# Chunked attention in a fused f32 layer: value products in quarters of the TensorE array, masked scores kept without zero blocks

## Chip, cores and metric

The kernel runs on one core of a Trainium2 chip. The time is the device time of one execution in microseconds (us); the time before is the median of three runs, 514.29 us (513.94 to 514.57).

## What is computed

One layer over 4 x 2048 = 8192 tokens of 256 features: attention inside chunks of 32 tokens, with a decaying causal mask and a gate, a residual and layer norm, then a gated feed-forward part with integer weights, a residual and layer norm again. Cut to what matters:

```python
Q = x @ W_q.T; K = x @ W_k.T; V = x @ W_v.T
mask = jnp.where(diff >= 0, decay ** diff, 0)          # 32 x 32, diff = i - j
S = jnp.einsum('bncd,bnkd->bnck', Qc, Kc) * mask       # per chunk of 32 tokens
O = jnp.einsum('bnck,bnkd->bncd', S, Vc).reshape(B, T, D)
gate = jax.nn.sigmoid(x @ W_g.T)
out = gate * O @ W_o.T + x
x = _layernorm(x + out)
h = silu(x @ wg.T) * (x @ wu.T);  x = _layernorm(x + h @ wd.T)
```

## The kernel before

**Tiling.** The tokens are worked in 16 blocks of 512 (`TB`), each 4 groups (`NG`) of 128 tokens. A group is two pairs (`PAIR` = 64 tokens), and a pair is two chunks of 32. Features lie in two halves of 128 (`KD`). Queries and keys are folded: `m` = W_q^T W_k, so the scores need only y = m x and x.

**Attention of one block.** `split_gate`, `split_y` and `split_v` make the gate, y and v by three products of split operands each (a high part, a low part, and a "gap" part after ScalarE has scaled the PSUM bank in place, line 540). `attn_scores` (L651) makes, for each group and feature half, two products of 128 rows x 64 columns: pair 0 into partitions 0 to 63 of the PSUM bank `ps`, pair 1 into 64 to 127. Then VectorE multiplies by the mask (L663), one operation for each half of the partitions. The result goes into the diagonal 64x64 blocks of `sT`, a tile of 128 x 4 x 128, of which there are two, used in turn; their off-diagonal blocks were zeroed once at the start (L282, GpSimd) and stay zero. `attn_values` (L673) makes, for each feature half `dc` and group, one product of the full array: v (128 tokens x 128 features) stationary, `sT` (128 tokens x 128 columns, half of them zero) moving. The bank `po` of one `dc` holds 512 tokens, and VectorE gates it into `goT[:, dc, :]` (L682) as soon as its four products are done, while PE makes the other `dc`. `token_parts` then makes the high part of goT (ScalarE, L479), the low part (GpSimd, L480) and, later, the gap part (VectorE, L486), and `split_out` multiplies by W_o (L521) and adds the residual (L744). The first block takes `attn_residual` instead (L704, L728).

**Feed-forward of one block.** `ffn_up` makes for each of six hidden chunks of 128 the products `fg` and `fu` (L833); ScalarE makes s = silu (L842), VectorE u = fu s (L853), ScalarE its high part (L858), GpSimd the low part (L859). `ffn_down` (L704 or L907) multiplies by the down weights. Between the two parts, normalized h is transposed by 32x32 blocks on VectorE (L785) and 16 DMAs of SyncE's queue (L792).

**Order.** The order on each engine is written out by hand: `in_turn` and `in_steady_turn` keep instructions in program order. Loop iteration b (b = 0 to 13) runs the feed-forward of block b beside the attention of block b + 2 and the v, y and gate products of block b + 3. On PE, in an iteration with all parts: hidden chunk 0, chunk 1, scores, chunk 2, v (high and low), chunk 3, v gap, **values**, y (high and low), chunks 4 and 5, y gap, gate (high and low), out (high and low), gate gap, out gap, down. On ScalarE after chunk 3: v copy, normalization of an earlier block (L433), go_hi, scaling of y. Blocks 0 and 1 have their values in the prologue; the last block's come in iteration 13, after which ScalarE has go_hi at once. PSUM has eight banks of 512 f32 per partition, handed out in turn by `bank`.

A second path, `wide_group`, runs only if a weight is too large for the split; with these inputs it doesn't run.

Of the kernel before, what the change touches and what calls it, by code (L numbers as in the profile page):

```python
# [47 lines left out]
F32 = mybir.dt.float32  # L48
# [4 lines left out]
ALU = mybir.AluOpType  # L53

P = 128
CHUNK = 32
PAIR = 2 * CHUNK
SQ = 32
TB = 512
NG = TB // P  # L60
# [16 lines left out]
def kernel(  # L77
# [15 lines left out]
    nc = tc.nc  # L93
    NT, D = x.shape
    H = ffn_gT.shape[1]
    KD = D // P
# [4 lines left out]
    const = ctx.enter_context(tc.tile_pool(name="const", bufs=1))  # L101
    setup = ctx.enter_context(tc.tile_pool(name="setup", bufs=2))
    xin = ctx.enter_context(tc.tile_pool(name="xin", bufs=2))
    work = ctx.enter_context(tc.tile_pool(name="work", bufs=2))
# [9 lines left out]
    def in_turn(ins):  # L114
        tc.keep_in_program_order(ins)

    def bank(name):
        return psum.tile([P, TB], F32, tag="ps", name=name)
# [73 lines left out]
    for n in WARM:  # L192
        nc.tensor.matmul(
            pi[:, :n],
            lhsT=nc.const_aps.tensor(0.0, [P, P]),
            rhs=nc.const_aps.tensor(0.0, [P, n]),
            start=True,
            stop=True,
# [56 lines left out]
    mask = const.tile([P, NG, PAIR], F32, tag="mask", name="mask")  # L255
    nc.vector.memset(mask, 0.0)

    def make_mask():
# [11 lines left out]
        for g in range(P // CHUNK):  # L270
# [5 lines left out]
                    chunk_mask[rows, :].unsqueeze(1).to_broadcast([CHUNK, NG, CHUNK]),  # L276
                )
            )

    sTs = [const.tile([P, NG, P], F32, tag=f"sT_{i}", name=f"sT_{i}") for i in range(2)]  # L280
    for sT in sTs:
        nc.gpsimd.memset(sT, 0.0)  # L282


    def integers(w, w_int, name):

# [46 lines left out]
    def in_steady_turn(ins):  # L333
        if steady:
            tc.keep_in_program_order(ins)
# [307 lines left out]
    def attn_scores(b, yT):  # L643
        xt = xTs.pop(b)
        halves = [slice(i * PAIR, (i + 1) * PAIR) for i in range(P // PAIR)]
        ps = bank(f"ps_{b}")[:, : NG * PAIR].rearrange("p (g c) -> p g c", c=PAIR)
        for g in range(NG):
            for fc in range(KD):
                for rows in halves:
                    tokens = slice(g * P + rows.start, g * P + rows.stop)  # L650
                    product = nc.tensor.matmul(  # L651
                        ps[rows, g, :],
                        lhsT=xt[:, fc, tokens],
                        rhs=yT[:, fc, tokens],
                        start=(fc == 0),
                        stop=(fc == KD - 1),
                    )
                    in_turn(product)
        sTs.append(sTs.pop(0))
        sT = sTs[-1]  # L660
        for rows in halves:
            in_steady_turn(
                nc.vector.tensor_tensor(sT[rows, :, rows], ps[rows], mask[rows], ALU.mult)  # L663
            )
        return sT.rearrange("p g c -> p (g c)")

    def attn_values(b, sT, v, sg):
        goT = work.tile([P, KD, TB], F32, tag="goT", bufs=1, name=f"goT_{b}")
        for dc in range(KD):
            po = bank(f"po_{b}_{dc}")  # L670
            for g in range(NG):
                cols = slice(g * P, (g + 1) * P)
                product = nc.tensor.matmul(  # L673
                    po[:, cols],
                    lhsT=v[:, g, dc * P : (dc + 1) * P],
                    rhs=sT[:, cols],
                    start=True,
                    stop=True,
                )
                in_turn(product)  # L680
            in_steady_turn(
                nc.vector.scalar_tensor_tensor(  # L682
                    goT[:, dc, :], sg[:, dc, :], 1.0, po, ALU.add, ALU.mult
                )
            )
        return goT
# [275 lines left out]
    sg, gate = attn_gate(0)  # L962
# [9 lines left out]
    v, copies = attn_v(0, with_m)  # L972
# [18 lines left out]
    sT = attn_scores(0, yT)  # L991
# [5 lines left out]
    goT = attn_values(0, sT, v, sg)  # L997
# [299 lines left out]
    def wide_group(start, weights):  # L1297

        wide_g, wide_u, wide_d = weights
        tokens = bass.ds(start, P)  # L1300

        def features(pool, tag, name):
            bufs = {"bufs": 1} if tag == "goT" else {}
            return pool.tile([P, KD, TB], F32, tag=tag, name=f"{name}_w", **bufs)[:, :, :P]

        def row(pool, tag, name):
            return pool.tile([P, NG, D], F32, tag=tag, name=f"{name}_w")[:, 0, :]

        def products(pb, pairs):
            for i, (lhsT, rhs) in enumerate(pairs):  # L1310
                nc.tensor.matmul(
                    pb, lhsT=lhsT, rhs=rhs, start=(i == 0), stop=(i == len(pairs) - 1)
                )
            return pb

        def part(dc):
            return slice(dc * P, (dc + 1) * P)

        xt = features(xin, "xT", "xT")
        nc.gpsimd.dma_start(xt, xT[:, tokens].rearrange("(k p) t -> p k t", p=P))  # L1320
        xn = row(xin, "x", "x")
        nc.gpsimd.dma_start(xn, x[tokens, :])
        sg, yT, goT, hT = (
            features(pool, tag, tag)
            for pool, tag in ((work, "sg"), (work, "yT"), (work, "goT"), (moved, "hT"))
        )
        for dc in range(KD):
            pg = products(
                bank(f"pg_w_{dc}")[:, :P],
                [(given["wg"][:, ec, part(dc)], xt[:, ec, :]) for ec in range(KD)],  # L1330
            )
            nc.scalar.activation(sg[:, dc, :], pg, AF.Tanh, scale=HALF)
            py = products(
                bank(f"py_w_{dc}")[:, :P],
                [(given["m"][:, ec, part(dc)], xt[:, ec, :]) for ec in range(KD)],
            )
            nc.vector.tensor_copy(yT[:, dc, :], py)
        v = row(work, "v", "v")
        pv = products(
            bank("pv_w")[:, :D], [(xt[:, ec, :], given["wv"][:, ec, :]) for ec in range(KD)]  # L1340
        )
        nc.vector.tensor_copy(v, pv)
        sT = sTs[-1]
        ps = bank("ps_w")[:, :PAIR]
        for i in range(P // PAIR):
            rows = slice(i * PAIR, (i + 1) * PAIR)
            products(ps[rows, :], [(xt[:, fc, rows], yT[:, fc, rows]) for fc in range(KD)])
            nc.vector.tensor_tensor(sT[rows, 0, rows], ps[rows, :], mask[rows, 0, :], ALU.mult)
        for dc in range(KD):
            po = products(bank(f"po_w_{dc}")[:, :P], [(v[:, part(dc)], sT[:, 0, :])])  # L1350
            nc.vector.scalar_tensor_tensor(
                goT[:, dc, :], sg[:, dc, :], 1.0, po, ALU.add, ALU.mult
            )
        h = row(norm, "h", "h")
        pa = products(
            bank("pa_w")[:, :D], [(goT[:, ec, :], given["wo"][:, ec, :]) for ec in range(KD)]
        )
        nc.vector.tensor_tensor(h, pa, xn, ALU.add)

        def normed(r, name, on_r=1.0):  # L1360
            st = small.tile([P, 6], F32, tag="st", name=f"st_{name}")
            mv = no_moments(name)
            nc.vector.bn_stats(st, r)
            nc.vector.bn_aggr(mv[:, 0, :], st)
            rstd = root(mv, name, on_r, groups=[0])
            nc.vector.reciprocal(rstd[:, :1], rstd[:, :1])
            nc.vector.tensor_scalar(
                r, r, mv[:, 0, 0:1], rstd[:, :1], ALU.subtract, ALU.mult
            )

        normed(h, "aw", HALF)
        nc.vector.tensor_scalar(h, h, 1 / HALF, None, ALU.mult)
        for dc in range(KD):
            pt = bank(f"pt_w_{dc}")[:, :P]
            nc.tensor.transpose(pt, h[:, part(dc)], ident)
            nc.scalar.copy(hT[:, dc, :], pt)
        uT = []
        for hc in range(KH):
            pg, pu = (
                products(  # L1380
                    bank(f"{name}_w_{hc}")[:, :P],
                    [
                        (w[hc * P // D][:, dc, hc * P % D : hc * P % D + P], hT[:, dc, :])
                        for dc in range(KD)
                    ],
                )
                for name, w in (("fg", wide_g), ("fu", wide_u))
            )
            s = work.tile([P, TB], F32, tag="s", name=f"s_w_{hc}")[:, :P]
            nc.scalar.activation(s, pg, AF.Silu)  # L1390
            u = acts.tile([P, TB], F32, tag="u_hi", name=f"u_w_{hc}")[:, :P]
            nc.vector.tensor_tensor(u, pu, s, ALU.mult)
            uT.append(u)
        r = row(work, "r2", "r2")
        rows = [piece[:, k, :] for piece in wide_d for k in range(TB // D)]
        pd = products(bank("pd_w")[:, :D], list(zip(uT, rows)))
        nc.vector.tensor_tensor(r, pd, h, ALU.add)
        normed(r, "fw")
        nc.gpsimd.dma_start(out[tokens, :], r)
# [77 lines left out]
```

## Time and profile before

| | |
|---|---|
| median of three runs | 514.29 us |
| the profiled execution | 515.19 us |
| its span, first to last instruction | 513.6 us |
| granted TensorE clock | 0.999 |
| value products (L673) | 256 records, 31.2 us busy |
| score products (L651) | 512 records, 18.4 us busy |
| masking (L663) | 32 operations, 13.0 us busy |
| gating (L682) | 32 operations, 22.0 us busy |

The profile is one execution. PE is TensorE's matmuls, PEld its weight loads, DVE VectorE, ACT ScalarE, POOL GpSimd, SPq the DMA queue of SyncE. A group's line gives line, engine, operation, output<-inputs, shapes and count, then busy time and mean duration in ns, then the idle time of the engine just before these instructions and what ended it. Matmuls are pipelined: a record's duration is longer than its share of the path, which the chain of work shows better. The chain gives start, length, and engine, tile and line of what the end waited for. A timeline line gives start, length, engine, line, operation, output<-inputs, shapes, count and, in brackets, the idle time before.

### The profile page before, as it was taken

To read this page: it belongs to the slowest core of one execution; us is meant where nothing else is said; L and a number is where in the kernel's file an instruction comes from. 1 tells how busy PE (TensorE), PEld (TensorE's weight loads), DVE (VectorE), ACT (ScalarE), POOL (GpSimd) and SP (SyncE) were. 2 spreads that over 40 slices of the span, in tenths; PEclk is the share of its full clock that TensorE was granted. 3 is DMA by queue.
4 is the path that set the end of the run, shared out by engine and by line. 5 is a ranking of instruction groups with operands and counts; after the bars stand their busy time and mean duration, and the time that the engine had idled before them with its cause. 6 is when DMAs were issued, how large, how long until landed. Compare 5 with 4: busy or idle time off the path is not lost.

```text
span 513.6 us, 9691 instructions
## 1 busy us (share of the span) xinstructions
PE 503.7 (98%) x3480; PEld 399.4 (78%) x3480; DVE 309.3 (60%) x725; ACT 373.1 (73%) x701; POOL 292.2 (57%) x324
## 2 busy tenths in 40 slices
PE   9999899999999999999999999999999999999995
PEld 5788677788878879787787878778787787877684
DVE  3977667564564647547474564647547464665654
ACT  4868686676868777686786868777686786766845
POOL 2835546554746557465464846557465564657764
PEclk9999999999999999999999999999999999999999
DMA  7720312112222122222212222122222211103112
GB/s 243 235 84 20 94 25 82 42 43 68 73 74 74 43 78 88 60 64 83 83 43 71 84 61 75 45 77 86 61 64 82 83 44 30 54 14 98 35 36 69
DMA packets 43315, 36.83 MB, mean 72 GB/s; under 512 B 4865, under 2 KB 39169, under 8 KB 43265
## 3 DMA queue, kind: packets, MB, share of 16 engines
q1 hardware_dynamic: 42144, 35.28, 22.9%
q10 hardware_dynamic: 1120, 0.92, 0.6%
q8 instruction: 28, 0.46, 0.4%
q14 instruction: 23, 0.18, 0.1%
HBM read 20.45 MB, written 8.39 MB: 56 GB/s over the span
## 4 chain that ended last, share of the span: by engine, by line
PE 74%; DVE 8%; ACT 7%; SPq 4%; issue 3%; POOL 2%; DMA 1%; DVEq 0%; ACTq 0%; POOLq 0%
PE fg L833 13%; PE fu L833 12%; PE fdn L704 11%; PE p_y L499 7%; PE p_g L499 7%; PE p_v L521 6%; PE p_o L521 6%; PE po L673 5%; SPq L792 4%; DVE u L853 3%; PE ps L651 2%; ACT s L842 2%; ACT h L433 1%; PE fdn L907 1%; DMA out_dram<-r 1%
## 5 line engine op out<-in xcount | busy, mean ns | idle before, releaser
L859 POOL TENSOR_TENSOR u_lo<-u,u_hi 128x512 f16<-128x512 f32 (+1 forms) x98 | 128.7, 1315 | 100.9 <-ACT u_hi L858 100.9
L853 DVE SCALAR_TENSOR_TENSOR u<-fu,s 128x512 f32<-128x512 f32 (+1 forms) x98 | 66.6, 680 | 127.1 <-ACT s L842 103.7
L858 ACT CAST u_hi<-u 128x512 fp32r<-128x512 f32 (+1 forms) x98 | 59.9, 612 | 85.0 <-DVE u L853 84.9
L833 PE MATMUL fg<-hT_hi,fg_hi 128*128 128x512 f32 (+1 forms) x196 | 71.1, 444 | 0.0
L842 ACT ACTIVATE s<-fg 128x512 f32<-128x512 f32 (+1 forms) x98 | 56.8, 580 | 6.3 <-PE fg L833 6.2
L833 PE MATMUL fu<-hT_hi,fu_hi 128*128 128x512 f32 (+1 forms) x196 | 60.6, 390 | 0.0
L833 PE MATMUL fg<-hT_lo,fg_lo 128*128 128x512 f16 (+1 forms) x196 | 58.2, 378 | 0.0
L833 PE MATMUL fu<-hT_lo,fu_lo 128*128 128x512 f16 (+1 forms) x196 | 57.4, 375 | 0.0
L480 POOL TENSOR_TENSOR go_lo<-goT,go_hi 128x512 fp32r<-128x512 f32 x30 | 38.7, 1313 | 26.3 <-ACT go_hi L479 26.3
L480 POOL TENSOR_TENSOR x_lo<-xT,x_hi 128x512 fp32r<-128x512 f32 x30 | 38.3, 1298 | 24.2 <-ACT x_hi L479 18.0
L744 DVE TENSOR_TENSOR h<-p_o,x 128x512 f32<-128x512 f32 x30 | 19.3, 686 | 42.5 <-PE p_o L521 32.4
L704 PE MATMUL fdn<-fd_hi,u_hi 128*128 128x256 f32 x312 | 44.7, 285 | 0.0
L833 PEld LDWEIGHTS fu<-hT_hi,fu_hi 128*128 128x128 f32 x196 | 36.5, 188 | 8.5
L833 PEld LDWEIGHTS fg<-hT_hi,fg_hi 128*128 128x128 f32 x196 | 34.7, 189 | 9.5
L704 PEld LDWEIGHTS fdn<-fd_hi,u_hi 128*128 128x128 f32 x312 | 39.0, 188 | 0.3
L433 ACT ACTIVATE h<-h,shift_h,scale_h 128x256 f32<-128x256 f32 x52 | 27.0, 590 | 16.8 <-POOL shift_h L396 16.8
L704 PE MATMUL fdn<-fd_lo,u_lo 128*128 128x256 f16 x312 | 38.6, 273 | 0.0
L810 POOL TENSOR_TENSOR hT_lo<-hT,hT_hi 128x512 f16<-128x512 f32 x28 | 35.5, 1290 | 3.7 <-ACT hT_hi L809 3.7
L833 PEld LDWEIGHTS <-fu_lo 128*128 128x128 f16 x196 | 19.2, 98 | 22.4 <-issue 0.3
L673 PE MATMUL po<-sT,v 128*128 128x128 f32 x256 | 31.2, 275 | 0.3 <-DVE sT L663 0.3
L704 PEld LDWEIGHTS <-u_lo 128*128 128x128 f16 x312 | 28.4, 98 | 3.9
L673 PEld LDWEIGHTS po<-sT,v 128*128 128x128 f32 x256 | 30.0, 192 | 0.7 <-PE p_v L521 0.5
(176 smaller groups left out, 1067.2 us busy)
## 6 DMA issues: line engine op xcount, KB each, us to landing
x<-in_x_dram SPq DMA_DIRECT2D x16, 512.0 KB, 3.5
xT<-in_xT_dram SPq DMA_DIRECT2D x15, 512.0 KB, 3.7
hT<-sq SPq DMA_DIRECT2D x224, 32.0 KB, 1.9
out_dram<-r SPq DMA_DIRECT2D x13, 512.0 KB, 3.1
out_dram<-r SPq DMA_DIRECT2D x7, 128.0 KB, 1.7
fg_int<-in_ffn_gT_dram SPq DMA_DIRECT2D x3, 256.0 KB, 7.0
fu_int<-in_ffn_uT_dram SPq DMA_DIRECT2D x3, 256.0 KB, 7.2
fd_int<-in_ffn_dT_dram SPq DMA_DIRECT2D x3, 256.0 KB, 5.9
```

Of the source, the lines that this page charges most:

```text
L433: nc.scalar.activation(r[:, g, :], r[:, g, :], AF.Identity, bias=shift[:, g : g + 1], scale=scale[:, g : g + 1],)
L480: in_turn(nc.gpsimd.tensor_tensor(lo[:, k, :], t[:, k, :], whole, ALU.subtract))
L499: nc.tensor.matmul(pb, lhsT=a[kind][:, k, i * P : (i + 1) * P], rhs=b[kind][:, k, :], start=kind + k == 0, stop=True, skip_group_check=True,)
L521: nc.tensor.matmul(pb[:, j * D : (j + 1) * D], lhsT=b[kind][:, k, g * P : (g + 1) * P], rhs=a[kind][:, k, :], start=kind + k + j == 0, sto ...
L673: product = nc.tensor.matmul(po[:, cols], lhsT=v[:, g, dc * P : (dc + 1) * P], rhs=sT[:, cols], start=True, stop=True,)
L704: product = nc.tensor.matmul(pb[:, j * D : (j + 1) * D], lhsT=part[:, g * P : (g + 1) * P], rhs=w, start=(i == 0), stop=(i == len(terms) - 1),
L810: nc.gpsimd.tensor_tensor(in_order[1], whole, in_order[0].bitcast(F32), ALU.subtract)
L833: product = nc.tensor.matmul(pb, lhsT=w[kind][:, dc, hc * P : (hc + 1) * P], rhs=hT[kind][:, dc, cols], start=(kind == kinds[0] and dc == ...
L842: in_turn(nc.scalar.activation(s, pg, AF.Silu, scale=SCALE / H_UP))
L853: nc.vector.scalar_tensor_tensor(u, pu, U_UP / H_UP, s, ALU.mult, ALU.mult)
L858: in_steady_turn(nc.scalar.copy(hi, u))
L859: nc.gpsimd.tensor_tensor(lo, u, hi.bitcast(F32), ALU.subtract)
```

## The change

The value products use quarters of the array. Token rows 0 to 63 of a group (pair 0) and rows 64 to 127 (pair 1) are multiplied apart, and each again for the two 64-feature halves of a feature half: four products of 64 rows x 64 columns, moving 64 columns, where one of 128 x 128 with 128 moving columns stood. Pair 0 writes one PSUM bank and pair 1 another, each bank holding both feature halves of its tokens: 8 blocks of 64 columns. The masked scores are a tile of 128 x 4 x 64 without zero blocks, written by one operation, from the pool `work` with two buffers; the two `sT` tiles and their zeroing go. The gating operation now takes one bank, that is both feature halves of one pair of every group, and writes `goT` in runs of 64. The path that doesn't run is changed in the same way.

```diff
-    sTs = [const.tile([P, NG, P], F32, tag=f"sT_{i}", name=f"sT_{i}") for i in range(2)]
-    for sT in sTs:
-        nc.gpsimd.memset(sT, 0.0)
...
-        sTs.append(sTs.pop(0))
-        sT = sTs[-1]
-        for rows in halves:
-            in_steady_turn(
-                nc.vector.tensor_tensor(sT[rows, :, rows], ps[rows], mask[rows], ALU.mult)
-            )
-        return sT.rearrange("p g c -> p (g c)")
+        sT = work.tile([P, NG, PAIR], F32, tag="sT", name=f"sT_{b}")
+        in_steady_turn(nc.vector.tensor_tensor(sT, ps, mask, ALU.mult))
+        return sT
+
+    def by_pairs(t):
+        return t.rearrange("p k (g r c) -> p (k g) r c", g=NG, c=PAIR)
+
+    def value_products(banks, v, sT, groups, order):
+        for dc in range(KD):
+            for g in groups:
+                for r, po in enumerate(banks):
+                    rows = slice(r * PAIR, (r + 1) * PAIR)
+                    for c in range(P // PAIR):
+                        dims = slice(c * PAIR, (c + 1) * PAIR)
+                        product = nc.tensor.matmul(
+                            po[dims, dc * len(groups) + g, :],
+                            lhsT=v[rows, g, dc * P + dims.start : dc * P + dims.stop],
+                            rhs=sT[rows, g, :],
+                            start=True,
+                            stop=True,
+                        )
+                        order(product)
 
     def attn_values(b, sT, v, sg):
         goT = work.tile([P, KD, TB], F32, tag="goT", bufs=1, name=f"goT_{b}")
-        for dc in range(KD):
-            po = bank(f"po_{b}_{dc}")
-            for g in range(NG):
-                cols = slice(g * P, (g + 1) * P)
-                product = nc.tensor.matmul(
-                    po[:, cols],
-                    lhsT=v[:, g, dc * P : (dc + 1) * P],
-                    rhs=sT[:, cols],
-                    start=True,
-                    stop=True,
-                )
-                in_turn(product)
+        banks = [
+            bank(f"po_{b}_{r}").rearrange("p (n c) -> p n c", c=PAIR)
+            for r in range(P // PAIR)
+        ]
+        value_products(banks, v, sT, range(NG), in_turn)
+        for r, po in enumerate(banks):
             in_steady_turn(
                 nc.vector.scalar_tensor_tensor(
-                    goT[:, dc, :], sg[:, dc, :], 1.0, po, ALU.add, ALU.mult
+                    by_pairs(goT)[:, :, r, :], by_pairs(sg)[:, :, r, :], 1.0, po, ALU.add, ALU.mult
                 )
             )
         return goT
```

More of the change, by code (lines that the diff above doesn't have):

```diff
@@ L1342, in wide_group @@
         nc.vector.tensor_copy(v, pv)
-        sT = sTs[-1]
+        sT = work.tile([P, NG, PAIR], F32, tag="sT", name="sT_w")
         ps = bank("ps_w")[:, :PAIR]
@@ L1347, in wide_group @@
             products(ps[rows, :], [(xt[:, fc, rows], yT[:, fc, rows]) for fc in range(KD)])
-            nc.vector.tensor_tensor(sT[rows, 0, rows], ps[rows, :], mask[rows, 0, :], ALU.mult)
-        for dc in range(KD):
-            po = products(bank(f"po_w_{dc}")[:, :P], [(v[:, part(dc)], sT[:, 0, :])])
+        nc.vector.tensor_tensor(sT[:, 0, :], ps, mask[:, 0, :], ALU.mult)
+        banks = [
+            bank(f"po_w_{i}")[:, :P].rearrange("p (n c) -> p n c", c=PAIR)
+            for i in range(P // PAIR)
+        ]
+        value_products(banks, v.unsqueeze(1), sT, range(1), free)
+        for i, po in enumerate(banks):
+            of_pair = slice(i * PAIR, (i + 1) * PAIR)
             nc.vector.scalar_tensor_tensor(
-                goT[:, dc, :], sg[:, dc, :], 1.0, po, ALU.add, ALU.mult
+                goT[:, :, of_pair], sg[:, :, of_pair], 1.0, po, ALU.add, ALU.mult
             )
```

## The prediction

> **What bounds the kernel now.** I read the page's busy shares first, then its chain of work that ended last, then that chain in a window of one loop iteration, then the groups of instructions by form, then the timelines where TensorE (PE) waits.
>
> ```profile
> PE 503.7 (98%) x3480; PEld 399.4 (78%) x3480; DVE 309.3 (60%) x725; ACT 373.1 (73%) x701; POOL 292.2 (57%) x324
> ...
> PE 74%; DVE 8%; ACT 7%; SPq 4%; issue 3%; POOL 2%; DMA 1%; DVEq 0%; ACTq 0%; POOLq 0%
> ```
>
> PE is the bound: nearly always busy and three quarters of the chain, at a granted clock of 0.999. A microsecond taken from PE in the loop is a microsecond of the span, unless another engine is late next. The chain in one iteration (start, length, what):
>
> ```profile
> 116.28 0.47 PE fu L833 x2
> 116.75 1.08 PE ps L651 x32
> 117.83 0.66 PE fg L833 x2
> 118.49 0.46 PE fu L833 x2
> ...
> 124.55 1.78 PE po L673 x16
> 126.33 1.86 PE p_y L499 x8
> ```
>
> The value products (po) stand on the path for 1.78 us per block. The scores (ps) already use half-width tiles, and give the price I need.
>
> ```profile
> L673 PE MATMUL po<-sT,v 128*128 128x128 f32 x256 | 31.2, 275 | 0.3 <-DVE sT L663 0.3
> L682 DVE SCALAR_TENSOR_TENSOR goT<-sg,po 128x512 f32<-128x512 f32 x32 | 22.0, 687 | 11.2 <-PE po L673 11.0
> L651 PE MATMUL ps<-yT,xT 128*64 128x64 f32 x512 | 18.4, 225 | 0.0
> L663 DVE TENSOR_TENSOR sT<-ps,mask 64x256 f32<-64x256 f32 x32 | 13.0, 406 | 0.4 <-issue 0.2
> ```
>
> Each f32 product leaves two records: 8 value products a block leave 16, 16 score products leave 32. A value record (128 moving columns) costs 1.78/16 = 0.111 us. A score record has half the columns, so one after another 32 would cost 32 x 0.056 = 1.78. They took 1.08: the start stamps come two by two, 6 to 7 ns apart, one pair every 58 ns. So the two column halves of the array run at the same time, and 16 rounds of 58 ns are 0.93. The rest of the 1.08, 0.15, is the way into the tiled mode; the way out is in the next row, where two fg records take 0.66 against 0.46 to 0.47 elsewhere: 0.20. A tiled stage costs its rounds plus 0.35.
>
> **What the Trainium skill says.** "TensorEngine Tiling (Array Packing)", Key Properties: a change of tiling mode drains the engine, and tiles load and multiply independently. The trace agrees: the 0.35 above, and the pairs. The same page, Gotcha 1: PSUM Pressure: different row tiles must write different banks; the edit has one bank per token half, so it obeys; no run here shows two row tiles. "TensorE: Matmul & The Clock Gate", Part 3, Measured speedup vs the span model: tiles of one round start about 4 ns apart and packing by rows and columns composes. The trace has 6 to 7 ns for columns, nothing for rows. "Runtime: NRT & Kernel Launch", Instruction fetch mechanics: an issue floor of about 20 cycles per instruction. The scores hold 4 instructions (two loads, two products) in 58 ns, 14.5 ns each; whether a faster pace lasts is not shown.
>
> **The change part by part.**
>
> *Products.* Removed: 16 records of 0.111. Added: 8 x 4 = 32 products, 64 records of 64 columns in quarter tiles. Four different quarters follow one another in program order, so a round has four records: 16 rounds of 58 ns are 0.93, plus 0.02 for two more starts, plus 0.35 of mode changes that po did not have: 1.30. Gain 1.78 - 1.30 = 0.48 per block. Bounds: at best the mode changes are half hidden, 1.12 (gain 0.66); at worst no row overlap, priced below.
>
> *Masking (L663).* Two 64x256 operations (0.85 together on the timeline) become one 128x256; other 128x256 rows on DVE take 0.40 to 0.41, so I take 0.42 and save 0.43 a block. Mostly DVE is idle anyway, but twice the masking stands in front of PE:
>
> ```profile
> 35.54 0.85 DVE L663 TENSOR_TENSOR sT<-ps,mask 64x256 f32<-64x256 f32 x2
> 36.53 2.02 PE L673 MATMUL po<-sT,v 128*128 128x128 f32 x16 [0.31 <-DVE sT L663]
> ```
>
> In block 1 the gap from the last record to po is 0.589 against 0.118 usually: 0.47 lost, 0.43 of it comes back. And in the loop, masking delays u, so u_hi, so ACT's scaling of p_v, which PE needs:
>
> ```profile
> 335.85 0.30 DVE sT L663
> 336.17 0.43 DVE sT L663
> 336.63 0.70 DVE u L853
> 337.35 0.62 ACT u_hi L858
> 337.97 0.49 ACT p_v L540
> 338.51 1.22 PE p_v L521 x8
> ```
>
> The gap ahead of the p_v gap products is 0.235 where nothing is late; it is 1.06, 0.58 and 0.31 at 91, 338 and 400 us (2.01 at 59 us, where sT is not in the chain). Cutting 0.43 from each gives back 0.43 + 0.34 + 0.07 = 0.84; I take 0.8 (bounds 0 and 0.9).
>
> *Gating (L682).* Still two operations of 512 per block. Each now walks eight runs of 64; the masking rows also write runs of 64 and cost no more than contiguous 256-element rows (406 against 401 to 413 ns), so 0.69 each (at most 0.75). But each reads a token half of all features, and its bank is full only with the last products: neither can start under the products, as the first did. Gating begins about 0.25 after the last product: 0.15 + 0.95 + 0.25 = 1.35 after po's start, and ends at 1.35 + 2 x 0.69 = 2.7; before it ended at 2.67 (124.39 to 127.06). go_hi of the first feature half, which needed only the first operation, now needs both. In the loop ACT reaches go_hi at 128.55, behind normalization, so this costs nothing. In block 0 the output products (L704) follow one product group later and now wait for gating: gain 0. In the last block ACT waits for gating already:
>
> ```profile
> 458.66 1.46 DVE L682 SCALAR_TENSOR_TENSOR goT<-sg,po 128x512 f32<-128x512 f32 x2
> 460.16 0.63 ACT L479 ACTIVATE go_hi<-goT 128x512 fp32r<-128x512 f32 x1 [0.16 <-DVE goT L682]
> 460.83 0.60 ACT L842 ACTIVATE s<-fg 128x512 f32<-128x512 f32 x1
> 461.52 0.69 DVE L853 SCALAR_TENSOR_TENSOR u<-fu,s 128x512 f32<-128x512 f32 x1 [1.39 <-ACT s L842]
> ```
>
> There both go_hi casts start after the second gating, so s, queued behind them, and its user u slip by about 0.47, and the chain runs on from u to a PE wait at 472: cost 0.5 instead of a gain (bounds 0 and 0.5).
>
> *What is late next.* PE arrives 0.48 earlier at the p_g gap products, where ACT's scaling had about 0.29 to spare and the shorter masking gives most of 0.43 more. One iteration (259 us) already stalls there. I charge 0.3 in all (bounds 0 and 1.3, 0.1 in each of 13 iterations).
>
> *Nothing else.* The two zeroing memsets (0.55 each on POOL at 2 to 3 us) lie under the input transfers. The second bank is needed 0.9 earlier; its earlier user, the score bank, was read some 3 us before. No DMA moves. The branch for wide integers does not run.
>
> Sum: 13 loop blocks x 0.48 = 6.2; block 1, 0.48 + 0.43 = 0.9; p_v waits 0.8; last block -0.5; p_g -0.3. Together 7.1. The profiled execution took 515.19 (span 513.6 and 1.6 around it), so 508.1; the median shown, 514.29, is 0.9 below that execution: **507.2**.
>
> **The rivals.**
>
> *Row halves take turns* (slower). The scores show only column halves side by side. If the two row halves alternate, there are 32 rounds of 58 ns: 1.86 + 0.35 = 2.21, 0.43 more than now. 13 x 0.43 = 5.6, block 1 even, last block 0.9, less 0.8 from the masking: +5.7, **520.0**. It decides once the stage exceeds 1.78, that is (1.78 - 0.35)/64 = 22 ns per record, before the masking's gain. For it: 29 ns per score record is the fastest lasting pace in the trace. Against: stamps 6 ns apart, and the skill's packing.
>
> *Instruction supply limits.* 128 loads and products must issue in 0.95. At 18 ns per record, midway between 14.5 and 22, the stage is 1.15 + 0.35 = 1.50, gain 0.28: 3.6 + 0.7 + 0.8 - 0.7 - 0.1 = 4.3, **510.0**.
>
> *A wait takes the place.* ACT's order from p_v to p_g is nearly closed; if PE stalls for half of what it gains in each iteration, 7.1 - 3.1 = 4.0, **510.3**.
>
> **How the numbers follow.** The likeliest case 0.65 (own range 504.5 to 509.5: both best bounds, half the mode cost hidden, give 7.1 + 13 x 0.18 + 0.5 = 10; the worst bounds of the small terms give 5), supply 0.10, wait 0.06, row halves 0.17, and 0.02 for a break-even between them. The likeliest case, supply, wait and break-even hold 0.8 within 504.5 to 514.5; the row case is left out. Faster by over 0.2% (1 us, about what a measurement of this kernel can tell from no change) 0.80, within it 0.03, slower 0.17.
>
> **What would show it.** Right: po as 64 records of 64x64 in about 1.1 us from first to last, starts in fours every 58 ns, the first p_y product about 0.1 late; masking as 16 operations of about 420 ns; iterations near 30.1 us instead of 30.6; both gating operations after the last product. Wrong: starts in pairs (row case), even spacing of 18 ns or more (supply), or new PE gaps ahead of the p_g or p_o gap products (wait). A gating operation much over 0.69, or mode changes costlier for quarters than for halves, would also break the sum.

## The result, and the profile after

The changed kernel takes 507.8 us (median of four runs, 506.66 to 508.91), against 514.29 before: a ratio of 0.9874, 95% interval 0.9847 to 0.9901. Its profiled execution took 507.07 us with a span of 505.5. The page of the profile after, its busy shares and its chain that ended last:

```profile
PE 493.7 (98%) x4248; PEld 387.0 (77%) x4248; DVE 301.1 (60%) x709; ACT 373.1 (74%) x701; POOL 291.4 (58%) x322
...
PE 69%; ACT 5%; DVE 4%; POOL 2%; SPq 2%; issue 2%; DMA 1%; DVEq 0%; ACTq 0%; POOLq 0%
```

PE is still the bound, with 10 us less of work and 768 more records. The groups by form, of after:

```profile
L688 DVE SCALAR_TENSOR_TENSOR goT<-sg,po 128x512 f32<-128x512 f32 x32 | 20.6, 684 | 16.1 <-PE po L670 16.1
L670 PE MATMUL po<-sT,v 64*64 64x64 f32 x1024 | 18.6, 221 | 0.0
L646 PE MATMUL ps<-yT,xT 128*64 128x64 f32 x512 | 18.4, 225 | 0.0
...
L655 DVE TENSOR_TENSOR sT<-ps,mask 128x256 f32<-128x256 f32 x16 | 6.3, 392 | 0.0
```

Gating costs the same per operation (684 ns against 687) though it walks runs of 64. Masking is 16 operations of 392 ns. The value products are 1024 quarter records, 64 a block. How a block's stage lies on PE, from the timeline of after:

```profile
212.11 1.10 PE L516 MATMUL p_v<-wv_gap,x_gap 128*128 128x256 f32 x8
213.14 1.16 PE L670 MATMUL po<-sT,v 64*64 64x64 f32 x64
214.23 0.73 PE L494 MATMUL p_y<-x_hi,m_hi 128*128 128x512 f32 x2
```

The stage takes 1.16 us from its first record to the end of its last. The steps between start stamps inside it, in ns, from the block at 243.22 us (the first seven rounds of the sixteen):

```
7 7 6 87 | 7 7 6 38 | 7 7 6 39 | 6 7 7 38 | 7 6 7 38 | 7 7 6 39 | 6 7 7 38
```

Four quarters start 6 to 7 ns apart, and from the second round on a round of four lasts 58 ns. From the last p_v record ahead of the stage to the third p_y record behind it, PE spends 1.875 us, against 2.362 before: 0.487 less.

The same trace by stretches, each counted between the first records of two score stages (the first score stage began 21.87 us after the span's start before, and 20.48 after):

| stretch | before | after | gain |
|---|---|---|---|
| scores of block 1 to those of block 2 | 19.28 | 18.53 | 0.75 |
| iteration b = 0 | 32.54 | 33.58 | -1.04 |
| b = 1 | 31.81 | 30.55 | 1.26 |
| b = 2 | 30.63 | 30.87 | -0.24 |
| an undisturbed later iteration | 30.61 | 30.07 | 0.54 |
| scores of block 2 to those of block 15 | 400.43 | 394.17 | 6.26 |
| from there to the end | 60.88 | 61.15 | -0.27 |

Two iterations are longer than before. That was the first thing to explain.

### The profile page after: what moved, and what is told of

Its sections match the earlier page's. It is cut to its first block, busy times and chain, and to the rows that moved or that the text cites. A ratio compares the mean times of both kernels' runs of the same rounds, so it can differ in the third digit from the quotient of the medians.

```text
span 505.5 us, 11205 instructions
## 1 busy us (share of the span) xinstructions
PE 493.7 (98%) x4248; PEld 387.0 (77%) x4248; DVE 301.1 (60%) x709; ACT 373.1 (74%) x701; POOL 291.4 (58%) x322
## 4 chain that ended last, share of the span: by engine, by line
PE 69%; ACT 5%; DVE 4%; POOL 2%; SPq 2%; issue 2%; DMA 1%; DVEq 0%; ACTq 0%; POOLq 0%
PE fg L839 14%; PE fu L839 13%; PE fdn L710 12%; PE p_y L494 6%; PE p_g L494 6%; PE p_o L516 6%; PE p_v L516 6%; PE po L670 2%; PE ps L646 2%; DVE u L859 2%; SPq L798 2%; PE fdn L913 1%; ACT s L848 1%; ACT h L428 1%; ACT u_hi L864 1%
## 5 line engine op out<-in xcount | busy, mean ns | idle before, releaser
L688 DVE SCALAR_TENSOR_TENSOR goT<-sg,po 128x512 f32<-128x512 f32 x32 | 20.6, 684 | 16.1 <-PE po L670 16.1
L839 PEld LDWEIGHTS <-fg_lo 128*128 128x128 f16 x196 | 14.0, 98 | 20.9 <-issue 12.9
## 6 DMA issues: line engine op xcount, KB each, us to landing
x<-in_x_dram SPq DMA_DIRECT2D x16, 512.0 KB, 3.9
xT<-in_xT_dram SPq DMA_DIRECT2D x15, 512.0 KB, 3.7
out_dram<-r SPq DMA_DIRECT2D x13, 512.0 KB, 3.1
```

The lines of the kernel that those rows point to most:

```text
L688: nc.vector.scalar_tensor_tensor(by_pairs(goT)[:, :, r, :], by_pairs(sg)[:, :, r, :], 1.0, po, ALU.add, ALU.mult)
L839: product = nc.tensor.matmul(pb, lhsT=w[kind][:, dc, hc * P : (hc + 1) * P], rhs=hT[kind][:, dc, cols], start=(kind == kinds[0] and dc == ...
```

## Experiments

All of them are timed beside runs of the kernel before on the same chip (medians 514.5 to 514.8); ratios are against those. All but the kernel called "before with one mask" start from the changed kernel with the small edit of the first experiment in it, and are compared with that.

### A small operation that slid (pinned)

In b = 0, PE waits 1.48 us longer than a usual gap ahead of the p_g gap products. VectorE at that place, timeline of before:

```profile
67.53 0.17 DVE L318 TENSOR_SCALAR wide<-top 128x9 f32<-128x9 f32 x1
68.32 0.69 DVE L853 SCALAR_TENSOR_TENSOR u<-fu,s 128x512 f32<-128x512 f32 x1 [0.62 <-ACT s L842]
68.93 0.68 DVE L486 SCALAR_TENSOR_TENSOR go_gap<-go_hi,goT 128x512 fp32r<-128x512 f32 x1
```

and after:

```profile
66.82 1.29 DVE L481 SCALAR_TENSOR_TENSOR go_gap<-go_hi,goT 128x512 fp32r<-128x512 f32 x2
68.02 1.27 DVE L313 TENSOR_SCALAR wide<-top 128x9 f32<-128x9 f32 x1
69.20 0.68 DVE L859 SCALAR_TENSOR_TENSOR u<-fu,s 128x512 f32<-128x512 f32 x1
```

`wide` marks the pieces of the weights that need the second path. It is not in the hand-written order, so it was free to move, and in the changed kernel it stands behind go_gap instead of ahead of u. There it took 1.27 us for 9 elements a partition instead of 0.17. GpSimd was at work on u_lo from 67.64 to 69.26, and wide ended 0.03 after that. The Trainium skill, "SBUF — State Buffer", section "Who interferes with whom", says that a VectorE operation of this kind can, in some forms, need the port pair shared with GpSimd, and that the later of the two then waits for the whole of the other. The traces agree: in twelve of the fourteen behind this document wide lasts anything from 0.17 to 1.32 us, and ends 0.03 after the GpSimd operation that it overlaps; in the two others that operation ends within 0.06 of wide's start, and wide takes 0.17. No run takes the GpSimd operation away. u of chunk 5, behind wide, was late, and so was ScalarE's scaling of p_g. The edit gives wide a fixed place ahead of u (cut to what matters):

```diff
+    def find_wide():
+        wide = const.tile([P, top.shape[1]], F32, tag="wide", name="wide")
+        in_turn(nc.vector.tensor_scalar(wide, top, EXACT, None, ALU.is_gt))
+        wides.append(wide)
+
     def count_wide():
...
-        wide = const.tile([P, top.shape[1]], F32, tag="wide", name="wide")
-        nc.vector.tensor_scalar(wide, top, EXACT, None, ALU.is_gt)
+        wide = wides[0]
...
             look_up(range(4, n_pieces))
+            find_wide()
```

> The changed kernel, with the small operation 'wide' (128x9 on VectorE, in no fixed order before) held at the place it had in the kernel before, ahead of u of chunk 4. Theory: in the changed kernel it slid behind go_gap, took 1.27 us beside a GpSimd operation and held u of chunk 5 back, which cost the first loop iteration 1.5 us of PE waiting ahead of the p_g gap products; here that wait is gone and the time is about 1.0 us less: 506.8. Rival: that wait comes from ScalarE's casts of the down weights in that iteration, and the time stays at 507.8.

Measured: 506.29 us (505.68 to 506.94), ratio 0.9842 [0.9829, 0.9855]. PE at the same place, timeline of after and then of this kernel:

```profile
72.63 0.73 PE L494 MATMUL p_g<-x_gap,wg_gap 128*128 128x512 f32 x2 [1.32 <-ACT p_g L535]
```

```profile
71.80 1.21 PE L500 MATMUL p_g<-x_gap,wg_gap 128*128 128x512 f32 x4 [0.26 <-ACT p_g L541]
```

In the traces the excess falls from 1.48 to 0.42 us and the iteration from 33.58 to 32.51. The slide cost 1.06 in the profiled execution; the medians are 1.5 apart, but the intervals of the two ratios still overlap a little. What is left of the wait, 0.42, I put down to the loop of ScalarE and VectorE that the next two kernels show; in this iteration it wasn't tested apart. The pin fixes the order, not the overlap: in two of the kernels below that have it (row halves in turn, full product first) wide still took 1.26 and 1.32 us.

### Quarter products with masking in two operations

```diff
-        in_steady_turn(nc.vector.tensor_tensor(sT, ps, mask, ALU.mult))
+        for rows in halves:
+            in_steady_turn(nc.vector.tensor_tensor(sT[rows], ps[rows], mask[rows], ALU.mult))
```

> As e5_pinned, but the masking again in two 64x256 operations (on the narrow sT). Theory of the prediction: the masking stands ahead of PE in block 1 (0.43 us) and ahead of the p_v gap products in some iterations (up to 0.8 us), so 1.2 us more than e5_pinned, 508.0, with PE waits ahead of the p_v gap products back. Rival: masking lies under PE's work and only the products matter: the same as e5_pinned within 0.3.

Measured: 512.52 us (512.27 to 513.51), ratio 0.9967 [0.9955, 0.9979]. That is 6.2 above the pinned kernel, far more than either side expected. The stage on PE is as short as in the pinned kernel (1.09 from its first record to the first of p_y), yet most iterations are back at 30.57 to 30.63. PE waits ahead of the p_g gap products, one line of this kernel's timeline of PE:

```profile
195.31 1.22 PE L500 MATMUL p_g<-x_gap,wg_gap 128*128 128x512 f32 x4 [0.15 <-ACT p_g L541]
```

Counted as what a gap exceeds its usual 118 ns, this wait is 0.28 to 0.32 us in each of eleven iterations. Inside the groups of gap products another 0.12 is lost at p_g and 0.1 at p_v, nearly all of it between the first record and the second. That is the same wait: wherever it is lost, the first product's weight load starts 0.05 after the end of ScalarE's scaling of the first bank, so it waits for that scaling. The sum, 0.51, is nearly the whole of what one masking operation gives back (30.59 to 30.07). The chain that ended last, in a window of this kernel, shows whose loop it is:

```profile
240.72 0.33 DVE sq L800
241.05 0.30 DVE sT L663
...
241.38 0.43 DVE sT L663
...
241.84 0.70 DVE u L868
...
242.56 0.62 ACT u_hi L873
243.18 0.30 ACT p_v L541
...
243.60 0.54 ACT p_v L541
244.15 0.52 ACT s L857
```

PE is not on it. The chain runs from the masking through u, its cast and the scaling of p_v, later through the scaling of p_g and p_o, the gate, h, its statistics, a few GpSimd operations and the normalization, and so to the next masking: a closed loop of ScalarE and VectorE with a period of 30.6 us, in which one of the two masking operations costs 0.43. In the pinned kernel the same part of an iteration runs on PE alone:

```profile
211.29 0.94 PE p_v L522 x8
212.23 1.09 PE po L676 x64
213.33 1.82 PE p_y L500 x7
```

### Before with one mask

The other half alone: the kernel before, its products as they were, and one masking operation.

```diff
-        for rows in halves:
-            in_steady_turn(
-                nc.vector.tensor_tensor(sT[rows, :, rows], ps[rows], mask[rows], ALU.mult)
-            )
+        in_steady_turn(nc.vector.tensor_tensor(sT[:, :, :PAIR], ps, mask, ALU.mult))
```

> The kernel before with its masking as one 128x256 operation that writes the first 64 columns of each group, value products unchanged in shape and number. The scores of pair 1 so stand in the columns of pair 0: the values of these tokens are left wrong, the work of every engine but VectorE is the same. Theory: before, TensorE was the bound in nearly every iteration (30.61 us) and the ScalarE-VectorE loop had the same period, so shortening the loop alone gives only the waits that were there: 0.43 in block 1, 0.5 at 91 us, 0.3 at 258 us, 0.34 at 338 us, 0.07 at 400 us, about 1.7: 512.6 us, iterations still 30.6. Rival: the masking by itself is worth the 6 us that the two-operation variant of the changed kernel lost: 508.3, iterations 30.1.

Measured: 511.27 us (511.09 to 512.0), ratio 0.9943 [0.9929, 0.9956]: 2.9 us faster than before, not 1.7, and not 6. Iterations are 30.55, so PE is the bound again; its chain in one of them:

```profile
243.50 0.94 PE p_v L521 x8
244.44 1.78 PE po L670 x16
246.23 0.48 PE p_y L499 x2
```

The waits named in the expectation went. The part that the theory missed is 0.06 us an iteration: before, the second record of the p_v gap products came some 0.06 to 0.1 late. It starts 0.274 to 0.279 after the end of the first bank's scaling in each iteration of before's loop, however early the first record started, and the weight load ahead starts 0.05 after that end. So PE waited for ScalarE at p_v in each of these iterations, though the gap ahead of the group doesn't tell it.

What the two kernels say together shows best in how early ScalarE's scaling of the first bank ended ahead of PE's first product that uses it, in a usual iteration (at 0.05 the product itself was waiting for it, and up to 0.1 its weight load was):

| | quarters | masks | p_v: early by | p_g: early by | iteration |
|---|---|---|---|---|---|
| before | no | 2 | 0.06 to 0.09 | 0.24 to 0.28 | 30.61 |
| two masks | yes | 2 | 0.06 to 0.1 | 0.05 | 30.59 |
| before, one mask | no | 1 | 0.63 | 0.71 | 30.55 |
| pinned | yes | 1 | 0.65 | 0.18 | 30.07 |

Before, PE's work and the ScalarE-VectorE loop had nearly the same period. Shortening either alone gives 0.02 or 0.06 an iteration, both together 0.54. By the ratios, quarters alone gave 1.7 us of 514.5, one mask alone 2.9, both with the pin 8.1: 3.5 came only from having both.

### Which quarters run together

Three orders or shapes of the same products. Row halves one after the other, as the rival supposed, by putting the row loop outside:

```diff
-        for dc in range(KD):
-            for g in groups:
-                for r, po in enumerate(banks):
+        for r, po in enumerate(banks):
+            for dc in range(KD):
+                for g in groups:
```

> As e5_pinned, but the products in another order: all of token rows 0 to 63 first, then all of rows 64 to 127; the two column halves still alternate. It is the prediction's slower rival made on purpose. Theory (four quarters run at a time because four different ones follow each other in program order): 32 rounds of 58 ns instead of 16, the stage 2.2 us instead of 1.3, 0.93 us more in each of 14 to 15 blocks: about 520, slower than the kernel before. Rival (PE picks ready products out of its queue, so that their order does not matter): the same as e5_pinned, about 507.

Row halves side by side, but with 128 columns (32 records), so without column halves:

```diff
-                    for c in range(P // PAIR):
-                        dims = slice(c * PAIR, (c + 1) * PAIR)
-                        product = nc.tensor.matmul(
-                            po[dims, dc * len(groups) + g, :],
-                            lhsT=v[rows, g, dc * P + dims.start : dc * P + dims.stop],
...
+                    product = nc.tensor.matmul(
+                        po[:, dc * len(groups) + g, :],
+                        lhsT=v[rows, g, dc * P : (dc + 1) * P],
```

> As e5_pinned, but tiles of 64 rows x 128 columns: two per group and feature half, row halves in turn, no column halves. Theory: row halves run at the same time too, but a load of 128 columns takes as long as it does in the full array (0.11 us per record in the kernel before), so 16 rounds of 0.11: 1.8 + 0.35, 0.85 more than e5_pinned in each of 15 blocks, about 519. Rival A (loads hide entirely, 16 rounds of 58 ns): about 507. Rival B (row halves take turns): 32 x 0.11 = 3.5, about 544.

And all records of one quarter ahead of the next:

```diff
-        for dc in range(KD):
-            for g in groups:
-                for r, po in enumerate(banks):
-                    rows = slice(r * PAIR, (r + 1) * PAIR)
-                    for c in range(P // PAIR):
-                        dims = slice(c * PAIR, (c + 1) * PAIR)
+        for r, po in enumerate(banks):
+            rows = slice(r * PAIR, (r + 1) * PAIR)
+            for c in range(P // PAIR):
+                dims = slice(c * PAIR, (c + 1) * PAIR)
+                for dc in range(KD):
+                    for g in groups:
```

> The changed kernel, pinned, with all 16 records of one quarter of the array ahead of those of the next. Theory: quarters work at the same time only when the program order brings different quarters next to one another, so 64 rounds of 58 ns instead of 16: 3.7 instead of 0.93, +2.8 a block, 15 blocks, 548 us. Rival: the engine looks far ahead and starts a later quarter's products while the first is busy: same as the pinned kernel, 506.3.

| | us | ratio | iteration | stage's first to last start |
|---|---|---|---|---|
| pinned, all four in turn | 506.29 | 0.9842 [0.9829, 0.9855] | 30.07 | 0.94 |
| row halves in turn | 515.81 | 1.0021 [1.0013, 1.0028] | 30.79 | 1.69 |
| row halves, 128 columns | 518.23 | 1.0071 [1.0043, 1.0098] | 30.86 | 1.73 |
| quarter after quarter | 539.26 | 1.0508 [1.0463, 1.0553] | 32.27 | 3.19 |

The stage on PE, from the timelines of these three in turn:

```profile
247.72 1.91 PE L676 MATMUL po<-sT,v 64*64 64x64 f32 x64
```

```profile
248.50 2.00 PE L674 MATMUL po<-sT,v 64*128 64x64 f32 x32
```

```profile
258.67 3.40 PE L676 MATMUL po<-sT,v 64*64 64x64 f32 x64
```

So the gain hangs on neighbouring products being of different quarters. In the order that the rival feared, the kernel is slower than before. The costs came out below the forecasts (0.72 an iteration, not 0.93; 2.2, not 2.8) because records overlap where one quarter gives way to another: in the last kernel the steps are 58 ns, but at each of the three changes three pairs start 3 to 6 ns apart. 64 rounds became about 55, and 32 about 29. So PE seems to look a few records ahead, not sixteen; a record doesn't tell its quarter, and this is read from the spacing alone. With 128 columns the two records of a pair start 7 ns apart as well. But a pair does the work of one round of four quarters and takes 112 ns instead of 58, which is what two such records would take in turn at 56 ns each (half of the 111 ns of a record with twice the moving columns in the kernel before). So these stamps don't show that the two work at the same time, and nothing is gained over taking turns. The forecast of 519 was near, but its reason, the length of the weight load, wasn't tried apart.

### What a mode change costs

One product of the full array (4 columns, overwritten later) is put into the stage: at its start, where the array changes mode anyway, or in its middle, where (with `dc == 1`) it forces one change out and one in.

```diff
         for dc in range(KD):
+            if dc == 0:
+                order(
+                    nc.tensor.matmul(
+                        banks[0][:, KD * len(groups) - 1, :4],
+                        lhsT=ident,
+                        rhs=sT[:, 0, :4],
...
```

> As e5_pinned, with one extra product per block that uses the whole array (128x128 stationary, 4 moving columns, into a place that is overwritten), ahead of the quarter products. The control of the next run: it adds a load and a short product but no change of mode. Expected 0.1 to 0.2 us per block, about 509.

> As e3a_full_first, with the extra product between the two feature halves of the quarter products, so that the stage leaves and enters the tiled mode once more. Theory: a way in and out costs 0.35 us: 15 x 0.35 = 5 us more than e3a_full_first, about 514. Rival (the 0.35 is not the mode change but the first load and the first products of the next stage, which the queue overlaps): within 1.5 us of e3a_full_first.

Measured: 508.4 us (507.69 to 509.31), ratio 0.9877 [0.9859, 0.9895], and 512.87 (512.14 to 513.34), 0.9957 [0.9943, 0.9971]. Timeline of the second:

```profile
246.19 0.69 PE L686 MATMUL po<-sT,v 64*64 64x64 f32 x32
246.81 0.39 PE L673 MATMUL po<-sT,ident 128*128 128x4 f32 x2
247.12 0.69 PE L686 MATMUL po<-sT,v 64*64 64x64 f32 x32
```

The two halves start 0.93 apart, twice as far as 8 rounds of 58 ns. From the record ahead of the stage to the third behind it the two kernels take 1.988 and 2.349: 0.36 for the pair of changes. Iterations differ by 0.33 (30.16 and 30.49), the medians by 4.5. The 0.35 of the prediction, read from the scores, holds for quarters.

### The end and the late transfer

Last block with values by feature half in four banks and four gating operations of 256, so that gating begins under the products:

```diff
+        if b == NB - 1:
+            for dc in range(KD):
+                part = slice(dc * NG, (dc + 1) * NG)
...
+                value_products(banks, v, sT, range(NG), in_turn, [dc])
+                for r, po in enumerate(banks):
...
+                            by_pairs(goT)[:, part, r, :],
+                            by_pairs(sg)[:, part, r, :],
...
+                            po[:, part, :],
```

> As e5_pinned, but in the last block alone the value products of each feature half have two banks of their own, and gating is four operations of 256, the first two under the second half's products. Theory: the last block's late gating holds back go_hi, s and u, so here this chain comes about 0.6 us earlier and the time is 0.5 us less than e5_pinned, 506.3. Rival: the end is bound by another chain (the chunk products and their splits), and the time is the same as e5_pinned.

Measured: 505.59 us (505.31 to 506.6), ratio 0.9832 [0.9819, 0.9846]. From the last scores to the end it takes 60.68 instead of 61.18. ScalarE there, timeline of after and then of this kernel:

```profile
451.68 1.15 ACT L474 ACTIVATE go_hi<-goT 128x512 fp32r<-128x512 f32 x2 [0.66 <-DVE goT L688]
452.74 0.58 ACT L848 ACTIVATE s<-fg 128x512 f32<-128x512 f32 x1
```

```profile
449.95 1.29 ACT L480 ACTIVATE go_hi<-goT 128x512 fp32r<-128x512 f32 x2
451.15 0.58 ACT L874 ACTIVATE s<-fg 128x512 f32<-128x512 f32 x1
```

The wait of 0.66 is gone, and the 0.5 is as expected. In the medians the gain over the pinned kernel (0.7) is within what the intervals leave open.

In b = 2, PE waited 0.68 at the p_g gap products, because ScalarE's cast of hT waited: the last of the 16 transfers of hT took 3.69 us from issue to landing (128.45 to 132.14), where the fifteen others took 1.8 to 1.9, and the store of an earlier block had just been issued behind it (129.15). So I moved that store to ScalarE's queue, after the casts:

```diff
-                store(b - 2, r_before)
+                waiting.append((b - 2, r_before))
...
             hTs[b + 1] = split_h(b + 1, moving)
+            for k, r_k in waiting:
+                in_turn(
+                    nc.scalar.dma_start(
+                        out[span(k, None), :].rearrange("(g p) d -> p g d", p=P), r_k
...
```

> As e5_pinned, but the store of a finished block is issued by ScalarE's queue after the hT_hi casts, not by SyncE's queue right behind the 16 hT transfers. Theory: in some iterations one of the 16 pieces of the last hT transfer lands 1.8 us late, behind the store's packets, and holds hT_hi, p_g scaling and PE (0.7 us in iteration 2); here no hT piece is late, and the time is 0.7 us less than e5_pinned, 506.1. Rival: PE has enough slack there in all other iterations and the later store holds the r2 buffer or ScalarE instead: the same or up to 1 us more.

and put all three edits together:

> The changed kernel with three repairs together: the small unordered operation pinned, the last block's values by feature half in four banks with four gating operations, and the store of block b - 2 issued from ScalarE's queue behind the hT_hi casts. If the three gains found one by one add up (1.4 and more of waits at 71 us go with the pin, 0.5 at the end, 0.3 to 0.7 at 133 us): 505.2 us, range 504.6 to 505.8. If they overlap (one wait takes what the other gave): 505.9, no better than the best single one.

The cast on ScalarE, timelines of after, of the kernel with the later store, and of the three together:

```profile
132.39 1.14 ACT L815 CAST hT_hi<-hT 128x512 fp32r<-128x512 f32 x2 [0.71 <-DMA out_dram<-r]
```

```profile
131.44 0.62 ACT L821 CAST hT_hi<-hT 128x512 fp32r<-128x512 f32 x1
```

```profile
131.26 0.62 ACT L841 CAST hT_hi<-hT 128x512 fp32r<-128x512 f32 x1 [0.55 <-DMA hT<-sq]
```

Measured: 505.96 us (505.83 to 506.29), ratio 0.9834 [0.9821, 0.9847], and 505.76 (505.3 to 506.61), 0.9835 [0.9821, 0.9848]. The first trace made me believe that the store was the cause: the wait at 132 us is gone in it, and the iteration is 30.16 instead of 30.69. But the last transfer is late there too, 128.16 to 131.19, and landed before the store was issued at 131.49. In the second trace the store is issued just as late, and the wait stands at 0.55, now put down to the hT transfer itself, which takes 3.57 us on the chain where the median of such transfers is 1.9. So it isn't the store.

The traces show something else beside each late transfer: a packet of an instruction queue. This queue's lines on the pages of before and of after:

```profile
q8 instruction: 28, 0.46, 0.4%
```

```profile
q8 instruction: 34, 0.56, 0.5%
```

Its packets have 16 KB and last 0.9 to 1.9 us. One ran from 130.14 to 131.10 in after, from 129.20 to 130.16 in the kernel with the later store and from 128.47 to 129.98 in that with all three, each while the last hT transfer was on its way. In the fourteen traces together 450 of 3136 hT transfers took over 2.3 us, and a packet of an instruction queue ran during every one of them; of the 2686 others that holds for 296. The six more packets of the changed kernel go with its 768 more products and as many more weight loads (98304 bytes for 1536 more records). No run changes these packets alone, so the cause is argued, not shown; but the change itself brings more of them, and in b = 2 one falls on the transfer that the cast waits for.

The three repairs don't add up: 505.8 is the "overlap" case of the expectation (505.9), and no better than the last block's edit alone.

### The removed memsets

```diff
+    idle = const.tile([P, NG, P], F32, tag="idle", name="idle")
+    for i in range(2):
+        nc.gpsimd.memset(idle, 0.0)
```

> The changed kernel, pinned, with two zeroing memsets of a 128 x 4 x 128 tile on GpSimd at the start, as before had. Theory: the 1.4 us by which the first scores came earlier in the changed kernel's profiled run is a difference between runs and not the memsets: 506.3 us, same as the pinned kernel within 0.6. Rival: the removed memsets gave the 1.4 us: 507.7.

Measured: 506.13 us (505.9 to 506.84), ratio 0.9841 [0.9828, 0.9855]: same as the pinned kernel. The first scores began at 21.34 us in its trace, at 20.68 in that of the kernel before with one mask, which has the memsets too, and between 20.48 and 21.83 in the traces of the kernels without memsets. The 1.4 us by which the profile after is ahead at that point is a difference between executions, not a gain.

## Why the prediction was right, and where its steps were not

The forecast was 507.2, and 507.8 was measured, inside the likeliest case's own range. Its main term, the products, was right in its working. That the sum came so near is in part luck: some 2.0 us of gain and 2.4 of loss that it did not have went against one another. Point by point, in the profiled execution and counted from the first scores (which leaves out the start-up):

| term of the sum | forecast | measured |
|---|---|---|
| 13 loop blocks, products | 6.2 | 6.6 (0.487 in a usual block, 0.69 in that of b = 1) |
| first wait ahead of p_v | 0.8 | 1.0 (0.82 to 0.24 at 91 us, 0.34 and 0.07 to 0) |
| wait inside the p_v gap products | not in it | 1.1 |
| p_g | -0.3 | -2.25 (-2.1 ahead of the gap products, -0.15 inside) |
| p_o gap products | not in it | -0.3 (0.02 an iteration) |
| many small steps | not in it | 0.1 |
| block 1 | 0.9 | 0.75 |
| last block | -0.5 | -0.27 |
| sum | 7.1 | 6.7 |

The terms of the loop (6.6 + 1.0 + 1.1 - 2.25 - 0.3 + 0.1) make up the 6.26 of its stretch in the table of the result.

- **The stage.** Right in every part: fours every 58 ns, 64 records in 1.16, 0.09 more on the way in, 0.487 gained. The 0.35 for a pair of mode changes was carried over from the scores and measured again. "Row halves take turns" would have needed another program order, "instruction supply limits" 18 ns a record where 14.5 came out.
- **Masking.** 0.39 instead of 0.42 each; right. But its place in the sum was wrong. "Mostly DVE is idle anyway" let me price it at 0.8 + 0.43, as a side gain. It is the condition of nearly all the rest: with two operations the quarters gain 1.7, not 8.1. The prediction had the pieces (ACT's order from p_v to p_g "nearly closed", some 0.29 to spare at p_g, where the table above has 0.24 to 0.28 with the weight load still to come off, "the shorter masking gives most of 0.43 more"), but it never put them together into a loop whose period could be held against PE's 30.6. "A wait takes the place" was the truth for the quarters without the masking, and stronger than priced: it took nearly all of 0.54 an iteration, not half. That the sum came out right owes to both edits being in one change. In block 1 the 0.43 did not add to the quarters' gain either: from its scores to those of block 2 it takes 18.80 with one masking operation and the old products, and 18.53 with quarters, whether masking is one operation or two.
- **p_g.** The failed step is "Nothing else" with the -0.3 beside it. In usual iterations nothing is lost. Ahead of its gap products three iterations lose 2.24 where before lost 0.14: 1.06 from the small operation that slid, 0.42 in the same place from the loop, 0.68 from the late hT transfer, 0.08 at 284 us. The slide was in none of my cases; I had gone through the operations that the diff names, and not those that the order leaves free. "No DMA moves" was right of the program's transfers alone: the packets of PE's instructions went from 28 to 34.
- **p_v.** The gap of 0.235 ahead of p_v was read rightly, but "where nothing is late" was wrong of it: the weight load waited for ScalarE there too, which showed only inside the group of records, between the first and the second, and in no listed gap. It gave 1.1 that I did not have. This and the p_g losses went against one another.
- **Last block.** Right in its sign and chain, 0.27 instead of 0.5. Counted from the last scores, gating still ended 0.1 earlier (7.27 against 7.37), and with both casts behind it s started 0.29 later (8.36 against 8.07), not 0.47. Gating by feature half takes the cost back.

## What to carry to other kernels

Where the profile shows one engine at 98%, ask how early the operands that it doesn't seem to wait for were ready. Here 0.06 to 0.09 us at p_v and 0.24 at p_g, in an iteration of 30.6, were the signs of a second loop with the same period, and a saving on the first engine alone was nearly lost. Shorten both, and measure each alone, or the gain is put down to the wrong edit. And look for operations that the hand-written order leaves free, since any change of the program can move them to a worse place.

## What the runs showed of the hardware that I had not expected

- Four 64x64 quarters of the array work at the same time for f32 products, 6 to 7 ns apart, at 58 ns a round of 64 columns: 14.5 ns a record, each with its own load. But only where the program brings them next to one another: at a change of quarter only three pairs of records overlapped.
- Row halves with 128 columns start in pairs too, but take 112 ns a pair, about as much as quarters taken two by two.
- A VectorE operation on 9 elements a partition took from 0.17 to 1.32 us, and in twelve of fourteen traces ended 0.03 after the GpSimd operation beside it.
- Every one of the 450 hT transfers that took over 2.3 us, instead of the usual 1.9, had a packet of an instruction queue beside it; more, smaller products bring more such packets (34 instead of 28).
